# A four-layer graph network on one core: the first two pairs in a written order, and reordered places around three layer boundaries

## The chip, the cores and the metric

One core of one Trainium2 chip runs the whole kernel. The metric is the device time of one execution in microseconds. The kernel before took 2540.08 us in the median of three runs (2536.53, 2540.08, 2540.33).

## The reference

x is 3327 x 256, adj is 3327 x 3327, symmetric in its pattern and sparse (about 1% of the entries are not zero, the diagonal is full). Four layers follow one another, each with a layer norm, a relu and a residual:

```
h = relu(layernorm(x));  x = x + layer(h)
layer 0:  adj @ (h @ W.T + b)
layer 1:  f = tanh(adj*adj) where adj > 0, top 700 of each row kept
          relu(f @ (tanh(h @ Wp + bp) @ Wg) + bg)
layer 2:  A = adj + I, scaled on both sides by its row sums ** -0.5
          relu(A @ (h @ W.T))
layer 3:  R = (adj + I) / row sums;  Xf = Xa = h;  twice:
          A  = top-0.9 attention of Xa (queries W1,W2; keys W3)
          Xf = R @ Xf;  Xa = A @ Xa;  Z += Xf @ U1.T + Xa @ U2.T
          layernorm(h + Z) * g + b
```

## The kernel before, in words

The nodes are padded to 26 tiles of 128. Tiles p and p + 13 form pair p; there are H = 13 pairs. Everything is float32. A product with adj is done in blocks of two by two with seven block products in place of eight. For that, sums of the four blocks of adj and sums of the four blocks of the nodes are needed. Line numbers are those of the kernel before unless "new" stands with them.

**Layers 0 to 2.** `products` (L593) loops over the 13 pairs p; each is a `Product`, whose columns are cut in three pieces c of 5, 4 and 4 tiles (CUTS). A piece is 7 matmuls of 128 columns for each of its k, so 35, 28 and 28 matmuls (L558). They accumulate in two PSUM banks. `Feed` brings the data: `load` fetches the four blocks ("quad") of piece (p, c) of adj by SP's DMA queue (L494) into three rotating buffers per block, and calls `count`; `add` (L510 to L513) makes four sums on VectorE, of which three go to buffers with two copies. `upto(n)` loads up to piece n + 2 and adds up to piece n + 1. `combine_nodes` (L342 to L351) makes the nodes' sums `tsa` on VectorE.

When a product has ended, `result` copies one bank by ScalarE (L574) and combines on VectorE (L579 to L584), and `finish` adds into x. Then `Pair` prepares the pair for the next layer: statistics (L366, L367), inverse root on POOL (L98, L100), scaling to xn (L380 on VectorE, L376 the second half of layer 0's pairs on ScalarE). Its stages on TensorE are called from within the next product at fixed places, "hooks", counted in matmuls of the product: `turn` (four transposes, L392, evicted to xT by ScalarE, L396) and one or two projections (L404), evicted by ScalarE (L437). WHERE gives the places; WHERE_FIRST those in the first product of a layer, where the layer before's last pair must still be turned and projected, and only its k = 12 part waits for that.

Layer 0 also counts the entries of adj above zero per row, to know whether the top 700 binds. `count0` (L660 to L667) adds the six blocks of a pair's first row tile into `pos_p`, which has two buffers, and folds it; `done0` sums over partitions with a one-column matmul `pc_p` (L672) and copies the counts (L673). For p = 0 and 1 this matmul is issued in `finish0` (L725 to L731), for others at hook 62. The first two products of layer 0 are special: `first_two` (L738) loads x, weaves turning and projecting of the 13 pairs with the six pieces of products 0 and 1 (order (0,0), (1,0), (0,1), (1,1), (0,2), (1,2)), and makes the key weights kq. It starts TensorE with 12 matmuls without use ("busy").

In layer 1 each loaded block is filtered: a relu-square on VectorE (L688) and a tanh on ScalarE (L689).

**Layer 3.** R @ Xf of pair 0 is done in two phases (FIRST_PHASES) of block products with slabs of adj or of stored sums (832 KB each, L1163 and L1165, three buffers); POOL adds the identity to some of them (L1167). `combine` (L1140 to L1148) makes the nodes' sums. Within that work lie pk_mean (L940, centring of the keys), logits (L974), exponentials (L999), search for the threshold on VectorE, transposes of the kept weights (L186, L189), their product (L197). A propagated pair passes `scale` (L1272), `turn` (L146) and `sums` (L1282). In the second step `finish3` (L1290) ends each tile: it loads z and x3, adds on POOL, multiplies and adds on VectorE, normalises and stores.

**What sets the order.** TensorE's instructions stand in the order in which the program emits them (a manual schedule of PE). The other engines' orders come from a scheduler which goes by priorities and by `issue_after`. [...]

Of the kernel before, what the change touches and what calls it, by code (L numbers as in the profile page):

```python
# [11 lines left out]
F32 = mybir.dt.float32  # L12
# [30 lines left out]
PE_ALONE = {mybir.EngineType.PE}  # L43


@with_exitstack
def kernel(
# [41 lines left out]
    nc.gpsimd.memset(minus_half, -0.5)  # L89
    warm = const.tile([P, 2], F32, name="warm")  # L90
# [49 lines left out]
    last_copied, last_turned, last_exp, last_found, last_scaled, last_key, last_sum = ([] for _ in range(7))  # L140
# [79 lines left out]
    def load_kq(w):  # L220
# [9 lines left out]
        def finish():  # L230
            pw = ps_tr.tile([P, 4, P], F32, tag="tr", name="pt_w1")
            for c in range(NC):
                nc.tensor.transpose(pw[:DA, c, :], a1s[:, c, :], ident)
            nc.scalar.copy(w1s, pw[:DA, :NC, :])
            p12 = new_acc("p12")
            for c in range(NC):
                nc.tensor.matmul(p12[:, c * DA : (c + 1) * DA], w1s[:, c, :], a2s, start=True, stop=True)
            nc.scalar.copy(kq[:, :, 1, :], p12[:, : NC * DA].rearrange("p (c e) -> p c e", c=NC))

        return finish  # L240
# [32 lines left out]
    def layers_0_to_2(again):  # L273
# [71 lines left out]
        def combine_nodes(rhs, a, b):  # L345

            t1, t2, t3, t4 = (ts[:, n, a:b, :P] for n in range(4))
            nc.vector.tensor_tensor(t1, rhs.blocks(0, 1, a, b), rhs.blocks(0, 0, a, b), ALU.subtract)  # L348
            nc.vector.tensor_tensor(t3, rhs.blocks(1, 1, a, b), rhs.blocks(0, 1, a, b), ALU.subtract)
            nc.vector.tensor_tensor(t2, rhs.blocks(1, 1, a, b), t1, ALU.subtract)  # L350
            nc.vector.tensor_tensor(t4, rhs.blocks(1, 0, a, b), t2, ALU.subtract)  # L351
# [5 lines left out]
        roots, applied = [], []  # L357

        def normed(name, x2, dst, split=False):
# [4 lines left out]
            with tc.issue_after(applied[-2].ins) if split and len(applied) > 1 else nullcontext():  # L364
                for i in range(2):
                    nc.vector.bn_stats(st[:, i, :], x2[:, i, :])  # L366
                    nc.vector.bn_aggr(mv[:, i, :], st[:, i, :])  # L367
            with tc.issue_after(roots[-1].ins) if roots else nullcontext():
                roots.append(rsqrt(r, mv[:, :, 1], EPS))
            for i in range(2):  # L370
                if split and i:
                    off = small.tile([P, 1], F32, tag="off", name=f"off_{name}")
                    nc.vector.scalar_tensor_tensor(
                        off, mv[:, i, 0:1], -1.0, r[:, i : i + 1], ALU.mult, ALU.mult
                    )
# [3 lines left out]
                else:  # L379
                    applied.append(nc.vector.tensor_scalar(  # L380
                        dst[:, i, :], x2[:, i, :], mv[:, i, 0:1], r[:, i : i + 1],
                        ALU.subtract, ALU.mult,
                    ))
# [26 lines left out]
        class Pair:  # L410


            def __init__(self, layer, p, rhs, x2):
# [4 lines left out]
                if layer == 3:  # L418
                    self.xn = pair_of(rhs.rows, p)
                    normed(self.name, x2, self.xn)  # L420
                    self.made = nc.vector.tensor_scalar(self.xn, self.xn, 0.0, None, ALU.max)
                else:
                    self.xn = work.tile([P, 2, D], F32, tag="xn", name=f"xn_{self.name}")
                    normed(self.name, x2, self.xn, split=layer == 0)
                last = {0: self.plain, 1: self.second, 2: self.scaled, 3: self.keys}[layer]
                self.stages = [self.turn] + ([self.hidden] if layer == 1 else []) + [last]
# [49 lines left out]
        class Feed:  # L476
# [3 lines left out]
            def __init__(self, layer, order, load_x, change=None, count=None, keep=()):  # L480
                self.layer, self.order, self.load_x = layer, order, load_x
                self.change, self.count, self.keep, self.made = change, count, keep, []
                self.quads, self.ready, self.x2, self.done = {}, {}, {}, [0, 0]

            def load(self, p, c):
# [12 lines left out]
                if self.count:  # L498
                    self.count(p, c, q)

            def add(self, p, c):
                a, b = CUTS[c]
# [7 lines left out]
                nc.vector.tensor_tensor(s1, a21, a22, ALU.add)  # L510
                nc.vector.tensor_tensor(a21, a11, a21, ALU.subtract)
                nc.vector.tensor_tensor(s2, s1, a11, ALU.subtract)
                nc.vector.tensor_tensor(s4, a12, s2, ALU.subtract)  # L513
# [3 lines left out]
                self.ready[p, c] = a11, a12, s4, a22, s1, s2, a21  # L517

# [70 lines left out]
        WHERE = {2: (60, 86), 3: (50, 64, 80), 6: (12, 22, 34, 46, 58, 70)}  # L589
        WHERE_KEYS = (74, 89)  # L590
        WHERE_FIRST = {2: (48, 66), 3: (44, 56, 70)}

        def products(layer, width, rhs, feed, finish, before, pair_after, following=None, counted=None, begin=None):  # L593
# [4 lines left out]
            n = 0  # L598
            for p in range(H):
# [4 lines left out]
                else:  # L604
                    prod = Product(layer, p, rhs, feed, width)
# [7 lines left out]
                    if counted:  # L613
                        hooks[62] = functools.partial(counted, p)
                    for c, (a, b) in enumerate(CUTS):
                        feed.upto(n)
                        cuts = [(a, b)]
                        if p == 0 and before and b == H:
                            cuts = [(a, b - 1), (b - 1, b)]
                        for cut in cuts:  # L620
                            if cut[0] == H - 1:
                                combine_nodes(rhs, *cut)
                            for at in prod.steps(c, *cut):
                                if at in hooks:
                                    hooks[at]()
# [60 lines left out]
        def filtered(a):  # L686

            nc.vector.scalar_tensor_tensor(a, a, 0.0, a, ALU.max, ALU.mult)  # L688
            nc.scalar.activation(a, a, AF.Tanh)  # L689
# [14 lines left out]
        if not again:  # L704
# [33 lines left out]
            def first_two(product):  # L738

                for a, b in ((0, 1), (1, 2), (2, 4), (4, 6), (6, 9), (9, 12), (12, 13)):  # L740
# [11 lines left out]
                    if a == 6:  # L752
                        feed.upto(-1)
                busy = bank("busy")
                for _ in range(12):
                    nc.tensor.matmul(busy[:, :P], ident, ident, start=True, stop=True)
                pairs = []
                prods = [product(p) for p in range(2)]

                def work_of(n):  # L760
                    p, c = order[n]
                    feed.upto(n)
                    yield from prods[p].steps(c, *CUTS[c])

                def some(steps, k):
                    for _ in range(k):
                        if next(steps, None) is None:
                            return

                ready = iter(())  # L770
                for p in range(H + 1):
                    while len(pairs) < min(p + 3, H):
                        pairs.append(Pair(0, len(pairs), rhs0, pair_of(x0, len(pairs))))
                    if p < H:
                        pairs[p].turn()
                    if p == 6:
                        with tc.issue_after(evicted[-1].ins):
                            finish_kq = load_kq(work.tile([P, 2 * D], F32, tag="y", name="kq_parts"))
                            load_weights()
                    some(ready, 8)  # L780
                    if p:
                        pairs[p - 1].plain()
                        for c, (a, b) in enumerate(CUTS):
                            if p == b:
                                combine_nodes(rhs0, a, b)
                                some(ready, 1000)
                                ready = itertools.chain(work_of(2 * c), work_of(2 * c + 1))
                    some(ready, 10)
                some(ready, 1000)
                finish_kq()  # L790
# [1016 lines left out]
```

## Time and profile before

| | us |
|---|---|
| median of three runs | 2540.08 |
| the profiled execution | 2537.56 |
| its span | 2535.7 |
| TensorE (PE) busy | 2493.2 (98%) |
| VectorE (DVE) busy | 2087.1 (82%) |
| ScalarE (ACT) busy | 1085.0 (43%) |
| GpSimd (POOL) busy | 302.1 (12%) |
| granted TensorE clock, mean | 0.997 |

How to read it: the span is the time from the first to the last instruction of the profiled execution. Busy times of the engines overlap. TensorE works nearly all of the span, so its idle stretches are what to look at: the view of waits lists them by the line that waited and the instruction that released it, and the timeline shows where each lies. Layer 1 begins at about 370 us, layer 2 at about 680, layer 3 at about 960, its second step at about 1820. A matmul of float32 leaves two records, a transpose one.

### The profile page before, as it was taken

To read this page: it belongs to the slowest core of one execution; us is meant where nothing else is said; L and a number is where in the kernel's file an instruction comes from. 1 tells how busy PE (TensorE), PEld (TensorE's weight loads), DVE (VectorE), ACT (ScalarE), POOL (GpSimd) and SP (SyncE) were. 2 spreads that over 40 slices of the span, in tenths; PEclk is the share of its full clock that TensorE was granted. 3 is DMA by queue.
4 is the path that set the end of the run, shared out by engine and by line. 5 is a ranking of instruction groups with operands and counts; after the bars stand their busy time and mean duration, and the time that the engine had idled before them with its cause. 6 is when DMAs were issued, how large, how long until landed. Compare 5 with 4: busy or idle time off the path is not lost. (4 is left out here: it accounts for less than half of the span.)

```text
span 2535.7 us, 47811 instructions
## 1 busy us (share of the span) xinstructions
PE 2493.2 (98%) x17953; PEld 2256.4 (89%) x17953; DVE 2087.1 (82%) x5538; ACT 1085.0 (43%) x2158; POOL 302.1 (12%) x485
## 2 busy tenths in 40 slices
PE   8999999999999999999999999999999999999998
PEld 7999999999999998888887888888888888888887
DVE  6667689888878778788879797884999999899995
ACT  3110123433111115565656565663655555555551
POOL 2000010000000001000000001000022211222222
PEclk9999999999999999999999999999999999999999
DMA  6577765555788866323132323133433343344333
GB/s 222 181 237 238 227 222 167 166 181 156 243 309 277 271 216 226 99 82 106 57 108 90 107 86 104 55 107 108 163 103 129 108 132 123 108 128 142 119 119 102
DMA packets 181773, 388.28 MB, mean 153 GB/s; under 512 B 19741, under 2 KB 78746, under 8 KB 181530
## 3 DMA queue, kind: packets, MB, share of 16 engines
q1 hardware_dynamic: 153210, 364.31, 43.9%
q10 hardware_dynamic: 28320, 20.80, 2.6%
q8 instruction: 143, 2.34, 0.4%
q14 instruction: 100, 0.82, 0.1%
HBM read 315.44 MB, written 67.89 MB: 151 GB/s over the span
## 5 line engine op out<-in xcount | busy, mean ns | idle before, releaser
L189 ACT COPY eT_a<-pt_a 128x512 f32<-128x512 f32 (+1 forms) x364 | 196.5, 555 | 375.8 <-PE pt_a L186 374.6
L197 PE MATMUL a<-h3a,eT_a 128*128 128x256 f32 x1352 | 324.1, 381 | 1.7 <-ACT eT_a L189 1.7
L197 PE MATMUL a<-vs,eT_a 128*128 128x256 f32 x1352 | 320.4, 381 | 1.8 <-ACT eT_a L189 1.8
L1061 DVE MAX8 cand_a<-w 128x8 f32<-128x128 f32 x1352 | 288.0, 279 | 4.3
L197 PEld LDWEIGHTS a<-h3a,eT_a 128*128 128x128 f32 x1352 | 244.0, 189 | 35.7 <-ACT eT_a L189 3.4
L197 PEld LDWEIGHTS a<-vs,eT_a 128*128 128x128 f32 x1352 | 244.7, 190 | 32.1 <-ACT eT_a L189 2.5
L558 PE MATMUL acc_a<-tsa,s_a 128*128 128x128 f32 (+1 forms) x2028 | 271.4, 275 | 0.3 <-DVE tsa L348 0.3
L558 PE MATMUL acc_a<-rhs,a_a 128*128 128x128 f32 (+1 forms) x2028 | 250.8, 276 | 2.2 <-ACT rhs L437 2.2
L558 PEld LDWEIGHTS acc_a<-tsa,s_a 128*128 128x128 f32 x2028 | 250.3, 192 | 1.4 <-DVE tsa L348 0.5
L558 PE MATMUL acc_a<-tsa,a_a 128*128 128x128 f32 x2028 | 250.5, 275 | 0.6 <-DVE tsa L351 0.6
L558 PEld LDWEIGHTS acc_a<-rhs,a_a 128*128 128x128 f32 x2028 | 238.4, 192 | 4.3 <-ACT rhs L437 2.8
L558 PEld LDWEIGHTS acc_a<-tsa,a_a 128*128 128x128 f32 x2028 | 239.3, 192 | 1.9 <-DVE tsa L351 1.0
L1057 DVE SCALAR_TENSOR_TENSOR w<-e_a,t_a 128x896 f32<-128x896 f32 x208 | 225.5, 1084 | 3.0
L999 ACT ACTIVATE e_a<-pl_a 128x1024 f32<-128x1024 f32 x260 | 184.7, 728 | 46.8 <-PE pl_a L974 40.6
L1167 POOL TENSOR_TENSOR slab3a<-slab3a,ident 128x128 f32<-128x128 f32 x100 | 95.1, 952 | 892.9 <-DMA slab3a<-in_adj_t_dram 327.9
L186 PE MATMUL pt_a<-ident,e_a 128*128 128x128 f32 x1352 | 198.7, 272 | 1.5 <-DVE e_a L1077 1.3
L1048 DVE SCALAR_TENSOR_TENSOR w<-e_a,t_a 128x3328 uint8<-128x3328 f32 x52 | 191.6, 3684 | 4.3
L1077 DVE SCALAR_TENSOR_TENSOR e_a<-e_a,all_least 128x3328 f32<-128x3328 f32 x52 | 191.6, 3685 | 1.8
L186 PEld LDWEIGHTS pt_a<-ident,e_a 128*128 128x128 f32 x1352 | 165.4, 141 | 30.7 <-ACT eT_a L189 2.7
L396 ACT ACTIVATE xT_a<-pt_a 128x512 f32<-128x512 f32 x52 | 30.8, 593 | 353.9 <-PE pt_a L392 307.5
L689 ACT ACTIVATE a_a<-a_a 128x640 f32<-128x640 f32 (+1 forms) x156 | 102.0, 665 | 169.9 <-DVE a_a L688 151.7
L1198 PE MATMUL f0a<-tsa,slab3a 128*128 128x128 f32 x1352 | 166.0, 276 | 2.8 <-POOL slab3a L1167 2.8
(248 smaller groups left out, 4234.3 us busy)
## 6 DMA issues: line engine op xcount, KB each, us to landing
slab3a<-s_dram SPq DMA_DIRECT2D x100, 832.0 KB, 4.4
a_a<-in_adj_t_dram SPq DMA_DIRECT2D x312, 256.0 KB, 4.1
slab3a<-in_adj_t_dram SPq DMA_DIRECT2D x79, 832.0 KB, 4.5
a_a<-in_adj_t_dram SPq DMA_DIRECT2D x156, 320.0 KB, 3.8
s_dram<-s_a SPq DMA_DIRECT2D x78, 256.0 KB, 4.7
s_dram<-s_a SPq DMA_DIRECT2D x39, 320.0 KB, 4.9
x_dram<-x_a ACTq DMA_DIRECT2D x39, 256.0 KB, 3.5
s_dram<-a_a SPq DMA_DIRECT2D x26, 256.0 KB, 5.1
```

The source lines that it names most:

```text
L186: nc.tensor.transpose(pt[:, j, :], e[:, k * P : (k + 1) * P], ident)
L189: last_turned.append(nc.scalar.copy(eT[:, : len(blocks), :], pt[:, : len(blocks), :]))
L197: nc.tensor.matmul(acc[:, :width], ready[g][:, j, :], rhs[:, k, :], start=(k == 0), stop=(k == T - 1))
L558: nc.tensor.matmul(self.acc[:, g, at : at + wide], quads[n][:, k - CUTS[c][0], :], t, start=(k == 0 and n in (1, 4)), stop=(k == H - 1 and ...
L689: nc.scalar.activation(a, a, AF.Tanh)
L999: last_exp.append(nc.scalar.activation(dst, src, AF.Exp, accum_out=parts[:, c : c + 1]))
L1048: nc.vector.scalar_tensor_tensor(junk, e, t, e, ALU.is_lt, ALU.mult, accum_out=got)
L1057: nc.vector.scalar_tensor_tensor(w[:, : (b - a) * P], eg, t, eg, ALU.is_lt, ALU.mult, accum_out=below[:, g : g + 1])
L1061: nc.vector.max(cand[:, 8 * k : 8 * k + 8], w[:, (k - a) * P : (k - a + 1) * P])
L1077: nc.vector.scalar_tensor_tensor(e, e, least, e, ALU.is_ge, ALU.mult, accum_out=st["kept"][:, m : m + 1])
L1167: nc.gpsimd.tensor_tensor(x[:, p, :], x[:, p, :], ident, ALU.add)
L1198: nc.tensor.matmul(self.accs[bank][:, c * P : (c + 1) * P], a, self.right(n, k), start=start, stop=last.get(bank) == (n, k), skip_group_ch ...
```

## The change

1. **Layer 0's start.** `first_two` becomes `first_two_in`, run under a manual schedule of VectorE, SP and ScalarE too. `Pair` is split into `measure` (statistics, inverse root) and `apply` (scaling) for that. All x loads come first, then three quads. The 13 pairs are turned and projected back to back; one add or one combine is put into each round from the sixth on. After that come the six pieces, each with its adds, loads and counts at written places. Counts are kept in a list (`to_count`) and taken from it one at a time; the last, of quad (1,2), is taken after `feed.upto(5)` and piece (0,2).
2. **First pair of layers 1 and 2.** The k = 12 part of its last piece is issued after the first piece of the second product. The hooks move to (58, 86) and (54, 72, 92).
3. **Layers 0 to 2.** The projection's hook goes from 86 to 84. Layer 1's tanh is issued after the last eviction emitted before it.
4. **Layer 3's entry.** The second phase takes its slabs in the order 5, 7, 6, 4; `combine` makes all 13 tiles at once, t3 before t2; the small constants are made at the kernel's start; the centring goes from hook 3 to 6 and the logits from 9 to 12; kT1 is allotted later. For the first row tile the propagated pair's scale, turn and sums go from (1, 3, 5) to (3, 5, 6).
5. **Second step.** At its first tile the scales of both open pairs go to hook 5, the turns and sums to 2, 5, 10, 14 of the following propagation. `finish_pair` (new) ends two tiles with one statistics block and one inverse root; the last pair still goes through `finish3`.

The core of the diff:

```diff
-        WHERE = {2: (60, 86), 3: (50, 64, 80), 6: (12, 22, 34, 46, 58, 70)}
+        WHERE = {2: (60, 84), 3: (50, 64, 80), 6: (12, 22, 34, 46, 58, 70)}
-        WHERE_FIRST = {2: (48, 66), 3: (44, 56, 70)}
+        WHERE_FIRST = {2: (58, 86), 3: (54, 72, 92)}
...
                         if p == 0 and before and b == H:
-                            cuts = [(a, b - 1), (b - 1, b)]
+                            steps(prod, c, a, b - 1)
+                            early.append(Product(layer, 1, rhs, feed, width))
+                            steps(early[0], 0, *CUTS[0], 12 * 7)
+                            combine_nodes(rhs, b - 1, b)
+                            steps(prod, c, b - 1, b, 1000)
...
             nc.vector.scalar_tensor_tensor(a, a, 0.0, a, ALU.max, ALU.mult)
-            nc.scalar.activation(a, a, AF.Tanh)
+            with tc.issue_after(evicted[-1].ins) if evicted else nullcontext():
+                nc.scalar.activation(a, a, AF.Tanh)
...
+                for _ in range(3):
+                    load()
+                pairs = [Pair(0, p, rhs0, pair_of(x0, p)) for p in range(H)]
...
+                pairs[0].measure()
+                for p in range(2):
+                    pairs[p + 1].measure()
+                    pairs[p].apply()
+                between = itertools.chain(add(), combining_nodes(rhs0, *CUTS[0]))
+                for p in range(H):
+                    pairs[p].turn()
+                    if p + 3 < H:
+                        pairs[p + 3].measure()
+                    if p + 2 < H:
+                        pairs[p + 2].apply()
                     if p:
                         pairs[p - 1].plain()
+                    if p > 4:
+                        next(between)
+                pairs[-1].plain()
+                run(between)
+                finish_kq = load_kq(work.tile([P, 2 * D], F32, tag="y", name="kq_parts"))
+                load_weights()
+                run(add())
+                combine_nodes(rhs0, *CUTS[1])
+                count()
+                work_of(0)
+                combine_nodes(rhs0, *CUTS[2])
+                run(add())
+                load()
+                finish_kq[0]()
+                work_of(1)
+                count()
+                run(add())
+                load()
+                count()
+                finish_kq[1]()
+                work_of(2)
+                run(add())
+                load()
+                work_of(3)
+                count()
+                count()
+                run(add())
+                last = feed.to_count
+                feed.to_count = None
+                feed.upto(5)
+                work_of(4)
+                last.pop(0)()
+                work_of(5)
...
-        FIRST_PHASES = (1, 2, 3), (5, 4, 7, 6)
+        FIRST_PHASES = (1, 2, 3), (5, 7, 6, 4)
...
             with tc.issue_after(left.made.ins):
-                combine(h3, ts, 0, H - 1)
-            combine(h3, ts, H - 1, H)
+                combine(h3, ts, 0, H)
...
-                    centred = {3: [lambda: centre(kT0, mean0(), "0")]}
-                    propagate_first(1, merged(centred, whole_run(steps, 9), plan))
+                    centred = {6: [lambda: centre(kT0, mean0(), "0")]}
+                    propagate_first(1, merged(centred, whole_run(steps, 12), plan))
                     run(find(0, 0, st0))
+                    kT1, ksum1 = new_keys(f"1{tag}", big)
...
-                    plan = merged(plan, {2: [p.scale, q.scale], 5: [p.turn], 6: [p.sums]})
-                    of_next = {3: [q.turn], 12: [q.sums]}
+                    plan = merged(plan, {5: [p.scale, q.scale]})
+                    of_next = {2: [p.turn], 5: [q.turn], 10: [p.sums], 14: [q.sums]}
...
-                        for j, k in ((1, m), (0, p)):
-                            if pair.last and not j:
-                                pair.ended()
-                            stores.append(finish3(k, ys.pop(k), both[:, j, :], f"{k}", pair.loaded))
+                        if pair.last:
+                            stores.append(finish3(m, ys.pop(m), both[:, 1, :], f"{m}", pair.loaded))
+                            pair.ended()
+                            stores.append(finish3(p, ys.pop(p), both[:, 0, :], f"{p}", pair.loaded))
+                        else:
+                            finish_pair(p, both, pair)
```

```diff
+        def finish_pair(p, both, pair):
...
+            for i in range(2):
...
+                with tc.issue_after(pair.loaded.ins):
+                    nc.sync.dma_start(zs[i], z_dram[:, m, :])
+                    nc.sync.dma_start(xs[i], x3_dram[:, m, :])
+                nc.gpsimd.tensor_tensor(zs[i], zs[i], ys.pop(m), ALU.add)
+            for i in range(2):
+                m = p + i * H
+                with tc.high_priority():
+                    nc.vector.scalar_tensor_tensor(zs[i], both[:, i, :], rinv[:, m : m + 1], zs[i], ALU.mult, ALU.add)
+            for i in range(2):
+                nc.vector.bn_stats(st[:, i, :], zs[i])
+                nc.vector.bn_aggr(mv3[:, i, :], st[:, i, :])
+            rsqrt(r, mv3[:, :, 1], EPS)
```

## The prediction

> **What bounds the kernel now.** I read the page's busy rows first, then TensorE's waits, then the timelines around each wait. PE is busy for 2493.2 of 2535.7 us:
>
> ```profile
> PE 2493.2 (98%) x17953; PEld 2256.4 (89%) x17953; DVE 2087.1 (82%) x5538; ACT 1085.0 (43%) x2158; POOL 302.1 (12%) x485
> ```
>
> No matmul is added or removed. The change can therefore gain only what PE idles, plus clock lost behind an idle stretch; it can lose without limit, by a new wait. PE's waits (line waited for: us in total, times, longest):
>
> ```profile
> PE prj_a L404 <- ACT xT_a L396: 4.3, 6, 1.3
> PE pt_a L392 <- DVE xn_a L380: 3.9, 3, 2.8
> PE pl_a L974 <- ACT e_a L999: 3.0, 1, 3.0
> PE f0a L1198 <- POOL slab3a L1167: 2.8, 1, 2.8
> PE acc_a L558 <- ACT rhs L437: 2.2, 1, 2.2
> PE pk_mean_0a L940 <- issue: 1.5, 1, 1.5
> ```
>
> The timeline places them: the xn and rhs waits at 14.43 and 29.52 us, the six prj waits in layer 1 (455 to 640), slab3a at 963.6, pk_mean at 967. From 1856 to 2432 PE never waits; that stretch can't gain. How the first segment ends (start, duration, instruction, idle before):
>
> ```profile
> 88.43 1.06 PE L558 MATMUL acc_a<-tsa,s_a 128*128 128x128 f32 x8
> 89.32 0.38 PE L233 MATMUL pt_w<-ident,kq_parts 128*64 128x128 f32 x2
> 90.32 0.66 PE L237 MATMUL p<-kq_parts 64*128 64x64 f32 x4 [0.61 <-ACT kq_parts L234]
> 91.33 0.16 PE L672 MATMUL pc<-ones,pos 128*128 128x1 bf16 x1 [0.24 <-ACT kq L238]
> 91.43 1.80 PE L558 MATMUL acc_a<-rhs,a_a 128*128 128x129 f32 x14
> ```
>
> Product p=2 starts at **91.43 us**; that is my mark for the first segment. Starts give the pitches: a 128-column matmul (two records) takes .222 us, four transposes .44 (44.99 to 45.43), a projection of four 256-column matmuls 1.73. So 35 matmuls take 7.8 us, 28 take 6.2, one pair's turn and projection 2.17.
>
> **First segment, work in the new order.** In the changed program's instruction order SP issues two 832 KB slabs of layer 3 before the first x (before: at 30.4 and 32.7 us), and POOL adds ident to one before the first rsqrt. The bytes before the second pair's end are 1.70 MB slabs + .26 weights + .52 x = 2.5 MB. The windows show 360 to 387 GB/s from 8 us on and less before; landing is about 9.3. DVE's written order measures pair 1 (.84) before it applies pair 0 (.4): first transposes ≈10.5 (before 7.35), pair 1 waits likewise for x 2 and 3 (≈12), first projection ≈12.4. Thirteen pairs then follow at PE's pace: per pair DVE needs 1.24 + .73 (one add or combine), ACT 1.6, POOL 1.05, all under 2.17. Pairs end at 12.4 + 1.73 + 12 × 2.17 = 40.2.
>
> Here a rule speaks against the change. The Trainium skill ("TensorE: Matmul & The Clock Gate", Part 1) says PE drops to half clock after an idle window of about 3.4 us. The rows say that less suffices: after the 2.75 us idle at 14.43 four transposes took .91 and a projection 2.64 (.44 and 1.73 warm), granted clock .72 for 12 to 16 us; after 2.19 us at 29.52 it was .72 for 32 to 36. But after the 2.81 us at 963.6 fourteen records took the warm time. The warming matmuls end at 6.9, so this idle is 3.6: by the rule just cold, by two rows of three too. I charge 1.5. (With x half a microsecond earlier the rule would charge nothing, the rows still 1.5.) **Pairs end X ≈ 41.7** (40 to 43.5).
>
> Then 2 × 7.8 + 4 × 6.2 + .7 (key weights) = 41.1 of work, E5 ≈ 82.8. DVE's adds, counts and loads, set row by row against PE's starts, keep ahead of it. Without further wait p=2 would start at 83.2: 8.2 gained.
>
> **The new wait.** PE's order puts the count matmul pc_1 before p=2. It reads pos_1, whose last count, of quad (1,2), the new code emits after the next load-and-add. In before this was done long ahead:
>
> ```profile
> 60.18 0.69 DVE L662 SCALAR_TENSOR_TENSOR pos<-a_a,pos 128x512 bf16<-128x512 f32 x1
> 61.48 0.23 DVE L667 TENSOR_TENSOR pos<-pos 128x128 bf16<-128x128 bf16 x1
> 86.21 0.68 DVE L727 TENSOR_TENSOR x_a<-x_a,y_a 128x512 f32<-128x512 f32 x1
> 92.06 0.82 DVE L662 SCALAR_TENSOR_TENSOR pos<-a_a,pos 128x640 bf16<-128x640 f32 x1
> ```
>
> In the changed DVE order it stands behind the finish of p=0 (ready only at E5 − 6.2), behind pos_2 (which needs the buffer that pc_0 frees, just after E5), and among the finish of p=1, which needs E5 and ACT's copy (.75). DVE idles some 5.5 us before all this and can't use it: its queue is in order. From E5, by starts of the same shapes: copy .75; four 128-wide u/y ops .8; y .53; pos_2's three counts .73 + .6 + .6; rs .14; quad (2,0)'s four adds 2.8; x_a .6; its bias .8; pos_1's counts 1.2; stats and aggregates .84; pos_1's three folds .8; one add of (2,1) .6: **11.8**. With pc_1 p=2 starts at 82.8 + 12.2 = 95.0, and 11.5 us idle costs 1.5 of clock: 96.5 in effect, **+5.1 against 91.43** (+3 to +7.5). Behind the wait PE holds p=2; its later adds and loads have some 7 us to spare, so the loss stays one-off.
>
> **First pairs of layers 1 and 2.** The k=12 part waits behind 35 matmuls of the next product, turn and projection move later: .44, .87, .34, .24 go. Each idle also costs about .17 of pipeline drain (453.12 + .89 of work, next start 455.21 with 1.03 called idle). **−2.2** (−1.5 to −2.6). The early add (1,0) is ready some 2 us ahead of its use.
>
> **tanh behind the last eviction.** In layer 1, ACT's in-order queue holds xT behind a tanh that waits for DVE:
>
> ```profile
> 454.04 0.63 ACT L689 ACTIVATE a_a<-a_a 128x512 f32<-128x512 f32 x1 [0.71 <-DVE a_a L688]
> 454.58 0.58 ACT L396 ACTIVATE xT_a<-pt_a 128x512 f32<-128x512 f32 x1
> 455.21 1.99 PE L404 MATMUL prj_a<-w2sa,xT_a 128*128 128x256 f32 x8 [1.03 <-ACT xT_a L396]
> ```
>
> In the new order xT precedes that quad's four tanh. The six waits sum to 4.35, with drain 5.4. What is late instead is the tanh, by .6, with about 14 us until its product. The earlier projection place (84 for 86) takes back .4 of cover. **−5.0** (−3.5 to −5.4).
>
> **Layer 3's entry.** pk_mean at place 6 and logits at 12 remove 1.53, pt_f's later scale .9, one .2 wait appears at the centring. The slab wait of 2.81 stays but for .35: POOL's kT_1 memsets still stand before the slab's add and wait for the x3 store (issued 954.9, landed 961.0). The combine in whole-width ops and constants made early are hidden by PE's 12 us of first-phase work. **−2.5** (−1.5 to −3.2; if the memsets move, −5).
>
> **Second step.** Scales at place 5 remove the 1.55 at 1821.3: **−1.6** (−1 to −1.8). finish_pair does one rsqrt per pair for two; DVE waited 21.3 us in 20 such places, but PE waits nowhere there: 0. If its cover goes, see rival B. Waits at 1778 (3.0) and 2499 (1.3), and the tail after PE's end (2522 to 2535.7), keep their instructions: 0.
>
> **Sum.** +5.1 − 2.2 − 5.0 − 2.5 − 1.6 = −6.2. The profiled execution took 2537.56 (span 2535.7 + 1.9), 2.5 under the median of 2540.08; its sum is 2531.4, against the median **2534**. The measurement tells about 0.2% (5 us) from no change, so this lies just beyond.
>
> **Rivals.**
> A. pos_1 isn't late, or pc_1 doesn't hold p=2. For it: counting alone is 2 us and DVE stands idle just before. Against: both orders are fixed. First segment −8.2, total −19.5: **2520.6**.
> B. finish_pair holds DVE. In the second step DVE is 92 to 95% busy, some 4 us free per pair; its high-priority multiply-add stands in order behind POOL's add, which waits for z loaded after the pair's last slab. A hold beyond 4 us reaches PE; at 5.5 each of twelve pairs adds 1.5, 18 in all: 2534 + 18 = **2552**. Against: z lands some 5 us after its issue, and the last slab needs 13 matmuls of PE after its own landing.
> C. The waits taken away in the later parts are filled by the next late thing by half (xT late for other reasons, the slab wait taking over pk_mean's): 5.65 less gain, **2539.5**.
>
> **Chances.** Forecast .55, its own range 2529.5 to 2538.5: .33 of it gains over 5 us, .20 stays within, .02 is slower with each cost at its end. A .13, faster. B .17, slower. C .15: .13 within, .02 faster. Faster .48, same .33, slower .19. The range runs from A's time, less 2, to 2546, which leaves out most of B.
>
> **What would show it.** First transposes near 10.5 and a half-rate stretch after; pairs back to back until about 42; pc_1 with an idle of about 11.5 us released by DVE's pos fold; p=2 near 95 us. No prj_a wait on xT_a in layer 1; pk_mean's wait gone, the slab3a wait still about 2.5; no PE wait from 1856 to 2432. I am wrong if p=2 starts below 88 or above 99, or if a new wait of over 2 us shows after 100 us.

## The result, and the profile after

| | before | after |
|---|---|---|
| median, us (8 runs each, same chip, in turn) | 2539.41 | 2546.24 |
| ratio to before, 95% interval | | 1.0027 [1.0016, 1.0038] |
| the profiled execution, us | 2537.56 | 2546.84 |
| its span, us | 2535.7 | 2545.0 |
| granted TensorE clock, mean | 0.997 | 0.993 |

The change makes the kernel slower by .27%. The forecast was 2534: the measured median is 12 above it and on the other side of no change. In the two profiled executions the difference is 9.3: the profile of before lies 1.9 under the median of its runs, that of after .6 over. Where an offset is given below, it is the start of the same TensorE work in one profile less its start in the profile of before. Single executions of before differ by 6 us (2535.9 to 2542.2), so offsets place a loss, and the medians size the whole.

The page's first row answers to the one shown of before: PE has the same 17953 instructions and 2.2 us more busy time in a span 9.3 longer.

```profile
PE 2495.4 (98%) x17953; PEld 2259.6 (89%) x17953; DVE 2094.8 (82%) x5534; ACT 1084.7 (43%) x2158; POOL 298.6 (12%) x463
```

TensorE's waits in after (line waited for: us in total, times, longest):

```profile
PE pc L720 <- DVE pos L715: 12.1, 2, 11.6
PE pt_a L415 <- DVE xn_a L403: 9.1, 3, 4.4
PE pl_a L1039 <- ACT e_a L1064: 3.0, 1, 3.0
...
PE pt_a L415 <- DVE h3a L458: 2.6, 3, 1.5
PE f0a L1263 <- POOL slab3a L1232: 1.5, 1, 1.5
...
PE f0a L1263 <- ACT xf_0a L1272: 1.3, 1, 1.3
```

(`prj` is the projection, `pt` the turn, `xn` a scaled pair, `h3a` the scaled pair that layer 2 hands to layer 3, `s_a` a sum of blocks of adj.) The six prj waits and pk_mean's are gone. At the top stands the count's wait that was forecast (11.6). In the second row two waits of over 4 us share one line; the timeline parts them. One lies at the start, which was forecast:

```profile
11.32 1.12 PE L415 MATMUL pt_a<-ident,xn_a 128*128 128x128 f32 x4 [4.30 <-DVE xn_a L403]
...
84.45 0.17 PE L720 MATMUL pc<-ones,pos 128*128 128x1 bf16 x1
96.25 0.19 PE L720 MATMUL pc<-ones,pos 128*128 128x1 bf16 x1 [11.63 <-DVE pos L715]
96.34 3.89 PE L598 MATMUL acc_a<-rhs,a_a 128*128 128x129 f32 x20
```

The other lies in layer 1, and nothing in the prediction speaks of it:

```profile
403.73 1.95 PE L598 MATMUL acc_a<-rhs,a_a 128*128 128x128 f32 x16
...
409.09 0.61 PE L598 MATMUL acc_a<-tsa,s_a 128*128 128x128 f32 x4
414.14 1.12 PE L415 MATMUL pt_a<-ident,xn_a 128*128 128x128 f32 x4 [4.45 <-DVE xn_a L403]
415.05 1.06 PE L598 MATMUL acc_a<-tsa,s_a 128*128 128x128 f32 x4
415.91 3.62 PE L598 MATMUL acc_a<-rhs,a_a 128*128 128x128 f32 x16
```

At 403.73 product p = 0 has just ended with its deferred k = 12 part, and the second piece of p = 1 begins. 26 matmuls (5.8 us; the expectations below say 24) later stands the hook that turns the pair of p = 0, and that pair isn't there yet. Behind the idle stretch 16 records take 3.41 us by starts (415.91 to 419.32) where warm ones take 1.78. The windows show it as a granted clock of .83 in a stretch that in before had no idle at all (start and end, us; busy of PE, PEld, DVE, ACT, POOL with counts; clock; DMA share; GB/s). First after, then before:

```profile
400.00:420.00 20.00, 15.55 (x115) 15.33 (x115) 15.90 (x32) 7.99 (x13) 1.28 (x2) 0.83 0.58 184
```

```profile
400.00:420.00 20.00, 20.00 (x174) 19.79 (x173) 17.58 (x33) 7.47 (x14) 1.00 (x2) 1.00 0.59 176
```

In before the same two points lay 13.6 us apart, and the turn waited for nothing:

```profile
389.05 2.40 PE L558 MATMUL acc_a<-rhs,a_a 128*128 128x128 f32 x20
...
402.68 0.60 PE L392 MATMUL pt_a<-ident,xn_a 128*128 128x128 f32 x4
```

What stands between the end of p = 0 and its pair's turn is seen on VectorE in after:

```profile
405.23 0.28 DVE L619 TENSOR_TENSOR u_a<-p_a,acc_a 128x128 f32<-128x128 f32 x1
...
409.37 0.68 DVE L731 SCALAR_TENSOR_TENSOR x_a<-y_a,x_a 128x512 f32<-128x512 f32 x1
...
410.70 0.74 DVE L386 BATCH_NORM_STATS2 st_a<-x_a 128x6 f32<-128x256 f32 x2
...
413.68 0.73 DVE L403 TENSOR_SCALAR xn_a<-x_a,mv_a,r_a 128x256 f32<-128x256 f32 x2 [0.91 <-POOL r_a L116]
```

ACT's copy (404.49 to 404.95), six combining operations, the two of the finish, statistics, POOL's root (412.28 to 413.64) and the scaling, with four filters of the next blocks (.74 each, by starts) and two adds in VectorE's queue among them: 10.4 us from 403.73 to the turn, against 5.8 of cover (the work that TensorE has in between).

The account of the two profiles, by offsets in us (the change in each stretch is the offset at its end less that of the row above):

| stretch | forecast | offset at its end | change |
|---|---|---|---|
| start to p = 3 of layer 0 | +5.1 | +6.3 | +6.3 |
| first pair of layer 1 | −2.2 with layer 2's | +14.4 | +8.0 |
| rest of layer 1 (tanh) | −5.0 | +9.6 | −4.8 |
| layer 2, its first pair above all | (above) | +13.3 | +3.7 |
| layer 3's entry, to the propagated pair | −2.5 | +10.8 | −2.6 |
| 1821 to 1831 | −1.6 | +10.1 | −.7 |
| from there to the end | 0 | +9.3 | −.8 |

The last row is made of two: the 1.26 wait at 2499 is gone, and the tail after PE's last group (2521.85 to 2535.7 in before, 2530.48 to 2545.0 in after) is .7 longer.

### The profile page after: what moved, and what is told of

The parts are those of the page before. It is cut to its first block, busy times and chain, and to the rows that moved or that the text cites. A ratio compares the mean times of both kernels' runs of the same rounds, so it can differ in the third digit from the quotient of the medians.

```text
span 2545.0 us, 47783 instructions
## 1 busy us (share of the span) xinstructions
PE 2495.4 (98%) x17953; PEld 2259.6 (89%) x17953; DVE 2094.8 (82%) x5534; ACT 1084.7 (43%) x2158; POOL 298.6 (12%) x463
## 4 chain that ended last, share of the span: by engine, by line
PE 58%; ACT 2%; issue 0%; DVE 0%; DMA 0%; POOL 0%; POOLq 0%; ACTq 0%; DVEq 0%
PE a L213 23%; PE f1a L1263 10%; PE f0a L1263 9%; PE pl_a L1039 6%; PE pt_a L202 6%; PE u L1347 2%; PE u L1317 2%; PE f L1198 1%; ACT junk_a L1102 1%; ACT junk_a L1097 0%; ACT e_a L1064 0%; PE pkq L268 0%; DMA x_dram<-x_a 0%; PE pt_a L162 0%; PE pt_f L162 0%
## 5 line engine op out<-in xcount | busy, mean ns | idle before, releaser
L1232 POOL TENSOR_TENSOR slab3a<-slab3a,ident 128x128 f32<-128x128 f32 x100 | 114.0, 1140 | 891.1 <-DMA slab3a<-in_adj_t_dram 335.2
```

The source lines that it names most:

```text
L1232: nc.gpsimd.tensor_tensor(x[:, p, :], x[:, p, :], ident, ALU.add)
```

## The experiments

My theory after the two traces: the deferral of the k = 12 part costs the time, since it brings the end of p = 0 close to a hook whose place is fixed. Rivals: the start alone makes the loss; or the parts that gain (tanh, layer 3) don't gain by themselves. Each ratio is to runs of before on the same chip, with its 95% interval.

**The deferral taken out of after.** p = 0 of layers 1 and 2 is again computed to its end before p = 1.

```diff
-        WHERE_FIRST = {2: (58, 86), 3: (54, 72, 92)}
+        WHERE_FIRST = {2: (48, 66), 3: (44, 56, 70)}
...
                             steps(prod, c, a, b - 1)
-                            early.append(Product(layer, 1, rhs, feed, width))
-                            steps(early[0], 0, *CUTS[0], 12 * 7)
                             combine_nodes(rhs, b - 1, b)
-                            steps(prod, c, b - 1, b, 1000)
+                            steps(prod, c, b - 1, b)
```

> The changed kernel with the deferral of the first pair's k = 12 part taken back (first pieces and hooks of layers 1 and 2 as before), all else as changed. Theory (the end of product 0 came 35 matmuls later, so its pair's next transposes, 24 matmuls on, waited): the waits of 4.45 us at 414 and 1.47 us at 717, the half-rate stretch after the first and the late loads of layer 2 go, the old waits of .44 + .87 + .34 + .24 return: about 11 us less than the changed kernel, 2535. Rival (the waits in layers 1 and 2 come from the new tanh order or are a backlog left by the start): at most 2 us less, the 4.45 us wait stays in some form.

Measured 2542.48, ratio 1.0006 [.9997, 1.0014]. The waits of 4.45 and 1.47 are gone, and layer 3 starts at +8.6 instead of +13.3: of .27% loss about .2% goes, 4 to 5 us, less than half of what was expected. The rest is taken back ahead of it. The longest of several new waits in the first pair of layer 1 is 1.79 us at 368.10, for h2T, and ACT's queue shows why: the copy h2T stands behind two tanh that wait for VectorE.

```profile
366.37 1.31 ACT L736 ACTIVATE a_a<-a_a 128x512 f32<-128x512 f32 x2 [1.02 <-DVE a_a L734]
367.59 0.82 ACT L482 ACTIVATE h2T_a<-hid_a,bpsa 128x256 f32<-128x256 f32 x2
```

With .36, .46, .87 and .52 after it the first pair loses some 3.5 us in this kernel as well.

**The turn later, the deferral kept.** Only p = 1's hooks are moved: turn from 60 (74 in layer 2) to 84, projection to 90.

```diff
-                    at = WHERE_KEYS if layer == 2 and p else (WHERE if p else WHERE_FIRST).get(len(todo), ())
+                    at = (84, 90) if early and p == 1 else WHERE_KEYS if layer == 2 and p else (WHERE if p else WHERE_FIRST).get(len(todo), ())
```

> The changed kernel, deferral kept, but in product 1 of layers 1 and 2 the turn and the projection (or keys) at places 84 and 90 instead of 60 and 84 (74 and 89). Theory: the turn then comes some 48 matmuls (10.7 us) after the end of product 0 and VectorE's chain to xn (9.9 us) fits: no wait over .5 us at 414 or 717, no half-rate stretch; about 9 to 11 us less than the changed kernel, 2536. Rival (backlog or tanh order): the wait moves with the turn, no gain beyond 3 us.

Measured 2543.6, ratio 1.0011 [1.0003, 1.0019]. In layer 1 the theory holds: of the first pair's waits only .43, .73, .47 and .52 are left, and layer 1 ends at +3.6 instead of +9.6. But 5.5 us come back in layer 2, where a wait for VectorE's adds and a slow stretch appear:

```profile
713.70 0.71 PE L598 MATMUL acc_a<-rhs,s_a 128*128 128x128 f32 x4 [2.36 <-DVE s_a L552]
714.24 0.60 PE L415 MATMUL pt_a<-ident,h3a 128*128 128x128 f32 x4
714.68 0.75 PE L598 MATMUL acc_a<-rhs,s_a 128*128 128x128 f32 x4
715.22 1.92 PE L598 MATMUL acc_a<-tsa,s_a 128*128 128x128 f32 x8
```

So the expectation for the total was missed: it supposed that layer 2 would do as layer 1 does, and there the adds are the next late thing.

**The deferral alone, on before.** All other parts are left as before.

```diff
-        WHERE_FIRST = {2: (48, 66), 3: (44, 56, 70)}
+        WHERE_FIRST = {2: (58, 86), 3: (54, 72, 92)}
...
+                    prod = early[0] if early and p == 1 else Product(layer, p, rhs, feed, width)
...
+                        if early and p == 1 and not c:
+                            n += 1
+                            continue
...
+                            early.append(Product(layer, 1, rhs, feed, width))
+                            steps(early[0], 0, *CUTS[0], 12 * 7)
+                            combine_nodes(rhs, b - 1, b)
+                            steps(prod, c, b - 1, b, 1000)
```

> The kernel before with the deferral alone (first product's k = 12 part behind the second's first piece, hooks 58, 86 and 54, 72, 92). Theory: at the second product's place 60, 24 matmuls after the end of the first, a new wait of about 4.4 us for xn in layer 1 near 402 with half-rate work after it, and about 1.5 us for h3a in layer 2 near 704; the four old waits (1.9 us) go: 6 to 9 us more than before, 2546. Rival (the deferral hurts only with the tanh order or with the shifted start): within 2 us of before.

Measured 2544.78, ratio 1.002 [1.0012, 1.0028], 4.9 us slower (6 to 9 were expected). The wait is there without the rest of the change, as long as in after:

```profile
401.95 0.61 PE L558 MATMUL acc_a<-tsa,s_a 128*128 128x128 f32 x4
407.01 1.11 PE L392 MATMUL pt_a<-ident,xn_a 128*128 128x128 f32 x4 [4.45 <-DVE xn_a L380]
```

The offset goes from +.3 to +7.0 at the first pair, falls to +3.4 by the last pairs of layer 1, since four of the six waits for xT are gone with no edit of the tanh (with PE 7 us later they had the time, as I read it), and is +5.3 at layer 3. So the parts aren't additive: most of what the tanh edit gains in after (4.8) the delay would have given anyway (3.6 here).

**The tanh edit alone, on before.**

```diff
-        WHERE = {2: (60, 86), 3: (50, 64, 80), 6: (12, 22, 34, 46, 58, 70)}
+        WHERE = {2: (60, 84), 3: (50, 64, 80), 6: (12, 22, 34, 46, 58, 70)}
...
+            with tc.issue_after(evicted[-1].ins) if evicted else nullcontext():
                 nc.scalar.activation(a, a, AF.Tanh)
```

> The kernel before with one part alone: layer 1's tanh issued after the last eviction, and the projection's place 84 for 86. Theory: the six projection waits of layer 1 (4.35 us, with drain 5.4) go, nothing else moves: 2535.4 to 2534, that is 4 to 5.4 us less than before. Rival (this is the part that hurts, by later sums or loads): the same or slower than before, with new waits for s_a or xn in layer 1.

Measured 2540.65, ratio .9995 [.9985, 1.0005]: no gain. Layer 1 does gain, 3.8 us from its first pair to its last, and all six prj waits are gone. Then waits of .82 and 2.14 come at the entry of layer 2 (before has .34 there), and its offset is back at 0. VectorE in this kernel, then in before:

```profile
684.83 0.69 DVE L662 SCALAR_TENSOR_TENSOR pos<-a_a,pos 128x512 bf16<-128x512 f32 x1 [4.03 <-DMA a_a<-in_adj_t_dram]
...
686.77 0.28 DVE L348 TENSOR_TENSOR tsa<-rhs 128x128 f32<-128x128 f32 x1
```

```profile
684.84 0.69 DVE L662 SCALAR_TENSOR_TENSOR pos<-a_a,pos 128x512 bf16<-128x512 f32 x1 [2.64 <-DMA a_a<-in_adj_t_dram]
```

The combination tsa, which p = 0's k = 12 part needs, stands behind a count whose block came no earlier than in before, although PE was ahead. The time saved in layer 1 is spent there. This trace loses 3 us more at layer 3's entry, where one idle of 4.70 us (967.26) stands for before's 2.81 and 1.53 and half rate follows it (24 records in 5.40 us against 2.86); why the idle falls otherwise was not taken apart.

**The same with that count put behind tsa.** In layer 2's first product the count is issued after the combination; the rest as in the tanh edit alone.

```diff
+                        held, real = [], feed.count
+                        if p == 0 and before and b == H and counted:
+                            feed.count = lambda *q: held.append(q)
                         feed.upto(n)
+                        feed.count = real
...
                                 combine_nodes(rhs, *cut)
+                                with tc.issue_after(combined[-1].ins):
+                                    for q in held:
+                                        feed.count(*q)
```

> The kernel before with the tanh order and place 84, and in layer 2's first product the count of quad (1,1) placed behind the sums tsa of k = 12 on VectorE. Theory (with the tanh order alone its gain of 2.4 us in layer 1 was lost where tsa stood behind that count, which waited for a landing at 684.8 that did not move): the wait of 2.14 us for tsa goes, key matmuls of layer 2 some 2.4 us earlier than before, total 2 to 3 us less, 2537. Rival (the landing holds the second product too): the wait moves to s_a or xn of the next product, no gain.

Measured 2538.28, ratio .9991 [.9984, .9997]. The 2.14 wait is gone, one of .89 for h3a at 702 is new, and layer 3 starts at −2.9. In the trace tsa is made at 680.06, 2.5 us ahead of the count, so the count no longer holds it. But that count's block came earlier too (its count starts at 682.54, not 684.83), so the landing isn't a fixed point; what sets it was not taken apart. The gain of about 1.6 us in the median has the sign of the explanation and not more: its interval overlaps that of the tanh edit alone, and this trace ends .7 behind that of before, since more half rate follows two of its idles that before has as well (2.81 us at 960.66: clock .86 in the 25 us around it, 1.00 in before; 3.01 us at 1777.39: last section).

**The last count early, in after.** It is taken before quad 5 is loaded and added, not behind piece (0,2).

```diff
-                last = feed.to_count
+                count()
                 feed.to_count = None
                 feed.upto(5)
                 work_of(4)
-                last.pop(0)()
                 work_of(5)
```

> The changed kernel, only the last count, of quad (1,2), taken before feed.upto(5) instead of after piece (0,2). Theory (pos_1 stands behind the finishes in VectorE's written order): pc_1 waits no more; but the four adds of quad (2,0) still stand behind pos_2, which waits for pc_0, so product 2 waits some 2.3 us for its first sum; product 2 in stride near 87, 8 to 11 us less than the changed kernel: 2536.5. Rival (any wait at that place is filled by the next late thing on VectorE): the whole 11 us stays as a wait for the sums of (2,0), under 3 us less.

Measured 2534.72, ratio .9979 [.997, .9988]. The 11.63 wait is gone; in its place stands one of 2.65 for the first add of the next quad:

```profile
89.15 0.94 PE L598 MATMUL acc_a<-tsa,s_a 128*128 128x129 f32 x6 [2.65 <-DVE s_a L549]
```

Layer 3 starts at +.6 instead of +13.3. The start of the change is thus worth a gain once its one misplaced count is moved, and the loss at the deferral (4.44 at 402.77) is still in this kernel.

**Layer 3's first slabs later, in after.** The first two slabs are issued behind the third x-and-quad load.

```diff
+                first_loads.append(feed.loaded)
...
+                first = not again and self.step == 0 and p == 0
+                with tc.issue_after(first_loads[-1].ins) if first else nullcontext():
```

> The changed kernel, only layer 3's first two slabs are issued after the third quad instead of ahead of all x. Theory (1.70 MB ahead of x in SP's queue delay it): first transposes near 7.8 instead of 11.3 us, the 4.3 us wait shrinks to under 1.5; the pairs, the pieces and pc_1 with its 11.6 us wait all move with it: 3 to 4 us less than the changed kernel, 2542.8. Rival (the later loads of the quads set the pace): first transposes earlier, but product 2 starts within 1 us of 96.3.

Measured 2541.17, ratio 1.001 [1.0001, 1.002], some 4 us less than after, as expected. The first transposes start at 7.13 with a wait of .57, and a second wait of 2.13 follows at 10.01, instead of 4.30 at 11.32. The count's wait stays at 11.64, and p = 2 comes 2.0 earlier. The slab wait at layer 3's entry is gone too, with .83 for pk_mean in its place. Layer 3 starts 3.5 earlier than in after.

**Layer 3's parts alone, on before** (items 4 and 5 of the change; layers 0 to 2 keep their code).

```diff
-        FIRST_PHASES = (1, 2, 3), (5, 4, 7, 6)
+        FIRST_PHASES = (1, 2, 3), (5, 7, 6, 4)
...
-                    propagate_first(1, merged(centred, whole_run(steps, 9), plan))
+                    propagate_first(1, merged(centred, whole_run(steps, 12), plan))
...
+                            finish_pair(p, both, pair)
```

> The kernel before with layer 3's part alone: constants early, second phase's order, whole combine, centring and logits later, scales later, finish_pair. By the marks of the changed kernel (pm to the first product of weights -1.45, pt_f -1.1, second step -.6, end about -.8): 3 to 4 us less than before, 2537. Rival (finish_pair holds VectorE, or entry's gain comes only with the changed order before it): no gain or slower, with a PE wait after 1856.

Measured 2540.74, ratio 1.0011 [1.0004, 1.0017]: slower, where 3 to 4 us less were expected. In layer 0 the trace loses 6.2: loads of adj with their counts and adds stand ahead of the first x's at the very start:

```profile
6.33 0.49 DVE L675 TENSOR_SCALAR pos<-a_a 128x640 bf16<-128x640 f32 x1 [5.48 <-DMA a_a<-in_adj_t_dram]
...
12.35 0.74 DVE L381 BATCH_NORM_STATS2 st_a<-rhs 128x6 f32<-128x256 f32 x2
...
14.72 0.41 DVE L395 TENSOR_SCALAR xn_a<-rhs,mv_a,r_a 128x256 f32<-128x256 f32 x1 [0.84 <-POOL r_a L115]
```

In before the statistics of the first x began at 3.97. Which part of the edit turns that order round is not shown; most of it is code at the end of the program, but it also makes the small constants at its start. Layer 3 gains: from +4.9 at its start to +.3 at 1821. Of these 4.6 us 1.6 are luck of this execution, the fastest of its 21: behind an idle of 3.00 us at 1780.70, which before has too, no half rate follows (last section). No wait of PE over .3 us lies behind 1832 in this kernel, nor in after: if finish_pair holds VectorE, PE doesn't see it.

**Three mended versions of after.** The first has the slabs later, the counts at other places and no deferral; the second defers in layer 1 only, with hooks 84 and 90; the third adds earlier hooks for p = 2 of layer 0 and issues kT1's memsets behind the slab's add.

```diff
-                last = feed.to_count
+                count()
-                feed.to_count = None
                 feed.upto(5)
                 work_of(4)
-                last.pop(0)()
                 work_of(5)
+                count()
+                count()
+                feed.to_count = None
```

> The changed kernel with the counts of (1,2) early and those of (2,0), (2,1) after the last piece, the slabs after the third quad, and no deferral in layers 1 and 2. Theory (parts add up): product 2 starts near 80 without a wait over .5, 11 us ahead of before; layer 1 and 2 about +1; layer 3 -3 to -4: some 13 us less than before, 2527.5. Rival (loads or VectorE give part of it back at layer 2's entry, where a landing held the kernel with the tanh order alone): 2531 to 2534, with a wait for tsa or s_a near 676.

Measured 2525.83, ratio .9949 [.9936, .9963]. Layer 0 ends at −7.9, in place of +6.3. A wait of 2.38 for xn remains at 86.39, and 1.70 for h3a in layer 2.

```diff
+                            if layer == 1:
+                                early.append(Product(layer, 1, rhs, feed, width))
+                                steps(early[0], 0, *CUTS[0], 12 * 7)
```

> As the one before (counts, slabs), but layer 1 keeps the deferral with product 1's turn and projection at 84 and 90; layer 2 without deferral. Theory (the deferral pays if the next pair's turn comes late enough): another 2 to 3 us less, 2525. Rival (layer 2's entry holds by its landing): the same as the one before within 1 us.

Measured 2523.78, ratio .9948 [.9934, .9962]. Layer 3 starts at −10.5 where the version before it had −6.3, but the medians can't be told apart; 1.6 us of the difference goes at the same idle of 3.00 us, which was followed by half rate in this trace and not in the other.

```diff
+                    if begin and p == 2:
+                        at = (24, 32, 42, 50, 60, 72)
...
+                    with nullcontext() if again else tc.issue_after(added[2].ins):
                         kT1, ksum1 = new_keys(f"1{tag}", big)
```

> The best so far (counts, slabs, layer 1's late turn, no deferral in layer 2) with product 2 of layer 0's hooks from place 24 on instead of 12, and kT_1's memsets behind the adds of slabs 5 and 7. Theory: the wait of 2.4 us at 87 goes with its share of slow clock, the slab wait of 1.5 us at layer 3's entry goes: 3 to 4 us less than the best so far, 2520. Rival (something as late stands behind each): within 1 us of it.

Measured 2521.95, ratio .9919 [.9905, .9932]: .8% under before, the lowest median here. The 2.38 wait and the slab wait are gone and layer 0 ends at −10.6. By the start of layer 3 it stands at −10.6, hardly earlier than the version before it: it led by some 3 us up to layer 2, and there 1.76 for tsa, behind the same count as above, came back at 674.87. The two traces end within .2 us of each other.

## Why the prediction was wrong

**The step that failed** is "First pairs of layers 1 and 2", put at −2.2. It asked whether the early piece's sums are ready and found 2 us to spare, which held (its only wait is .73 for the eviction of a projection that falls inside it). It did not ask who waits for the end of p = 0. That end is the start of a chain of about 10 us, and the chain's own end has a fixed place, hook 60 of p = 1 (74 in layer 2). The deferral moved the start behind the first piece of p = 1 and left the place: 13.6 us of cover became 5.8. Measured in after: +8.0 in layer 1, of which 7.5 at the turn (4.45 idle with its .17 of drain, and 2.9 of half clock: 2.5 of them from 414.14 to 419.32, against 402.68 to 405.35 for the same records), and .5 ahead of it, where .54 and .73 for rhs replace the .44 and .87; +3.7 in layer 2, where 1.47, .52 and .23 are the first pair's and .55 and .54 come at 783 and 828. In these two stretches the profile is nearly 14 us off the forecast, out of the 15 by which it missed the sum. Not all of that is the deferral's own. Put into before alone it costs 4.9 us, and taken out of after it gives back 4 to 5, so against −2.2 it is wrong by some 7 of the 13 us by which the medians missed; the first pair of layer 1 loses 3.5 us in after without it too. The deferral alone shows the loss directly, and moving the hook takes layer 1's away. Why layer 2's later two waits come was not tested.

**The start** was right in mechanism and close in size: first transposes 11.3 (10.5 said), pairs' end 42.8 (41.7), the count behind the finish of p = 1, an idle of 11.63 (11.5), p = 2 at 96.3 (95.0), 1.5 of half clock (20 records in 3.73 against 2.23). +6.3 against +5.1 is mostly the later x. The early count shows that the placing of this one item decided the sign of the whole first segment. On the clock, the Trainium skill's 3.4 us ("TensorE: Matmul & The Clock Gate", Part 1) fits the idles of 4.30, 4.45 and 11.63, which were all followed by half clock. The rows stay against it as a threshold: after the 2.36 at 713.70 in the kernel with the later turn, eight records took 1.71 by starts where .89 is warm, while after the 2.65 with the early count all ran warm; and the idle of 3.00 in the last section is below 3.4 and was followed by half rate in nine traces of thirteen. The same page's free-running window would let the price depend on where an idle falls in it; the runs show that the price differs (last section), not why.

**The tanh** gave −4.8 for −5.0 in after, but for a reason only half mine. "What is late instead is the tanh" was checked inside layer 1 only. Alone, the edit gives its gain back at layer 2's entry, behind a count; in after, where PE is 9.6 late, no such wait appears. The agreement in size is partly luck, since the delay alone takes four of the six waits away.

**The entry** gave −2.6 for −2.5 in other pieces: pk_mean's 1.53 and pt_f's .9 are gone, the slab wait fell to 1.54, and a new one of 1.25 for xf_0a came at 992. The slab wait was forecast to stay at about 2.5, so this sum is right partly by luck. **The second step** gave .7, not 1.6: a wait of 1.04 at 1831 replaces the 1.55 at 1821. That the 1.26 at 2499 would go was missed.

**The rivals.** A fell: the count was late. B fell: no PE wait appears from 1856 on. C, gains filled by the next late thing, is true of the tanh alone, of two places in layer 3 (1.25 and 1.04), and of layer 1's first pair when the deferral is taken out; the 4.45 in after is not of this kind. The losing case I lacked was a second place of the kind that I had found at the count: something late because of where it stands. My own sign of error, a new wait over 2 us after 100 us, is the one that came.

**Open.** Why the scheduler puts slabs or quads ahead of x when layer 3's code changes; the cause of the 1.25 for xf_0a (the new order of the slabs is my guess; it comes with layer 3's parts, since the kernel with these alone has it too, 1.26 at 983.98). Neither was taken apart.

## What to carry to other kernels

When a stage is put later, ask not only whether its inputs are ready but what its end releases, and whether that has a fixed place; write down the cover in microseconds before and after. In an order written by hand, each ready item behind a late one is as late: the one count behind a finish cost 11.63 us of idle, more than the back-to-back pairs gained. A gain ahead of a block's landing is lost there when the landing doesn't move with it (684.83 against 684.84 with the tanh edit alone), so cost an edit up to the next such point and not to the end of its own layer. And before a difference of 1 to 3 us between two traces is put down to an edit, compare the half rate behind the idles that both have.

## What the runs showed of the hardware that was not expected

The same idle, in front of the same instructions, has no one price. All thirteen traces have one of 3.00 or 3.01 us shortly before layer 3's second step, where a logits matmul waits for ACT's exponentials. The 36 records behind it took 4.10 us in four traces, 5.6 to 5.7 in eight (before and after among them) and 7.15 in one. Ten us around it in the first mended version, in before, and in the tanh edit with the count put behind (columns as above, the clock third from the end):

```profile
1765.20:1775.20 10.00, 6.99 (x59) 5.81 (x56) 9.70 (x17) 9.21 (x22) 0.65 (x3) 1.00 0.31 109
```

```profile
1774.00:1784.00 10.00, 6.99 (x43) 5.70 (x42) 9.72 (x17) 8.95 (x21) 0.65 (x3) 0.83 0.18 71
```

```profile
1773.10:1783.10 10.00, 6.99 (x33) 5.71 (x32) 9.72 (x17) 8.96 (x21) 0.65 (x3) 0.70 0.19 75
```

So the length of an idle does not settle what it costs: by these 36 records 0, 1.6 or 3.1 us more. Likewise, after the 11.63 us at the count's wait 20 records took 3.73 in after (96.34 to 100.07), but 4.43 in the kernel with the later turn (95.24 to 99.67), and the six behind them .67 and 1.13. A slow stretch need not begin at the restart: after the 2.36 idle at 713.70 four transposes took .44, as warm, and the half rate came 1.5 us later. Single profiled executions of unchanged stretches agreed within .02 us over many products (all of layer 0 after p = 3 at +6.33), so single executions part at few places. The idle of 3.00 us is one of them; how much of the 6 us between executions of before comes from such places was not measured.
